# A PixArt block on one core: the MLP rows of batches 4 to 15 turned in 32x32 blocks by VectorE and regrouped through DRAM, a batch ahead, in place of TensorE transposes

## The chip, the core and the metric

The kernel runs on one core of a Trainium2 chip. The metric is the device time of one execution in microseconds (us). The kernel before takes 749.11 us (median of 3 runs, 748.86 to 749.24).

Engines are called as in the profile: PE is TensorE (matmuls; PEld its weight loads), DVE is VectorE, ACT is ScalarE, POOL is GpSimd, SP is SyncE, which here only issues DMAs.

## The reference

One transformer block on `x` of 16 batches x 256 tokens x 256 features: self-attention, cross-attention and an MLP, all in float32. The change lies in the MLP:

```
x_norm2 = modulate(_ln(x), shift_m, scale_m)      # t * (1 + scale) + shift, per batch and feature
h = jax.nn.gelu(x_norm2 @ W_mlp1 + b_mlp1)        # 256 -> 1024
h = h @ W_mlp2 + b_mlp2                           # 1024 -> 256
x = x + gate_m[:, None] * h
```

`_ln` takes mean and variance over the 256 features of a token.

## The kernel before

Every matmul operand is split into a high part in fp32r and a low part, the rest; a product is three matmuls (high x high, high x low, low x high). Attention takes the first 560 us or so. There the 32 units (16 self, 16 cross) run over a hand-written plan, and the result of each cross-attention goes to a DRAM tensor `x2d`. The rest is the MLP stage, the loop at the end of the function over `chunks`, 4 chunks `c` for each of 16 batches `b`. In the text, chunk number `i` is 4b + c, and a step is one pass of this loop.

What stands in a step, in order: `mlp_gelu` of chunk i+1 (ACT makes `hf` and `hh` from the PSUM tile `ph`, GELU in float32 and in fp32r; POOL makes `hl` = hf - hh); in steps 4b, for b from 2 to 14, `mlp_T(b+1)`; `mlp_first` of chunk i+2 (12 matmuls of 128x256 into `ph`, two PSUM buffers); `mlp_second` of chunk i-1 (12 matmuls into `s` or `st`: even batches use `s`, odd ones `st`). With the last chunk of a batch, `mlp_second` also has DVE multiply by the gate (`mt`), add the residual (`y`), and SP store `y` to `out`. So PE has 96 matmuls a batch, beside `mlp_T`.

`mlp_T(b)` of before: PE turns the normalised rows `xn_m` by 4 transposes (matmuls against the identity) into the PSUM tile `psT_m`; DVE scales and shifts them into `xTf_m` (2 instructions); ACT makes the high part `hi` from the same PSUM tile (2 instructions, into `wkch` or `wqch`, by turns); DVE subtracts to the low part `lo` (`wkcl` or `wqcl`). The first `mlp_first` that reads hi and lo of batch b+1 stands in step 4b+2.

The rows come there by `mlp_load` (SP reads x2d into `x`), `mlp_bias` (POOL adds `cb`), `mlp_stats` and `pow` (DVE statistics `st_m`, `mv_m`; POOL makes 1/sqrt, `rs_m`) and `mlp_apply` (DVE: (x - mean) * rs, 2 instructions, `xn_m`), spread over the steps of the batch two before. `mlp_residual` (DVE) makes `xmg`, `mlp_gates` (SP) loads the gate rows `gm`, the same 2 KB of DRAM to all 128 partitions.

What sets the order: PE, DVE, POOL and SP issue in the order of the code. ACT does so up to step 22 (`ACT.on = i < E_['AP']`, 23); behind that the scheduler places its instructions. Buffers of a tag are reused in turn: `x` has 5, `ph` 2, `hh` and `hl` 3.

Of the kernel before, what the change touches and what calls it, by code (L numbers as in the profile page):

```python
# [10 lines left out]
F32 = mybir.dt.float32  # L11
F32R = mybir.dt.float32r
AF = mybir.ActivationFunctionType
ALU = mybir.AluOpType
AX = mybir.AxisListType

P = 128
# [4 lines left out]
def pixart_block(  # L22
# [8 lines left out]
    B, N, H = x.shape  # L31
# [3 lines left out]
    NT = N // P  # L35
    KC = H // P
# [21 lines left out]
    ACT, DVE, POOL, SP = (InOrder(e, True) for e in (nc.scalar, nc.vector, nc.gpsimd, nc.sync))  # L58

    const = ctx.enter_context(tc.tile_pool(name="const", bufs=1))  # L60
    work = ctx.enter_context(tc.tile_pool(name="work", bufs=2))
    dram = ctx.enter_context(tc.tile_pool(name="dram", bufs=2, space=bass.MemoryType.DRAM))
    psum = ctx.enter_context(tc.tile_pool(name="psum", bufs=2, space=bass.MemoryType.PSUM))

    LONG, SHORT = "gen", "tr"
    ps_turn = [0]

    def ps_gen(name, tag=None):


        if tag is None and ps_turn[0] is not None:
            ps_turn[0] ^= 1
            tag = (SHORT, LONG)[ps_turn[0]]
        tag = tag or SHORT
        return psum.tile([P, 512], F32, tag=tag, name=name, bufs=2)
# [25 lines left out]
    def tok(ap, b):  # L101
        return ap[b].rearrange("(p t) h -> p t h", p=P)
# [24 lines left out]
    cpT = const.tile([P, 12, B], F32, name="cpT")  # L127
    bqkv = const.tile([P, 6, B], F32, name="bqkv")
    sc1 = const.tile([P, 2, 2, B], F32, name="sc1")
# [302 lines left out]
    def mm3_tok(dst, xT, t, W, kn=KC, start=True, stop=True):  # L432
        n = 0
        for k in range(kn):
            for a, b in ((xT[0], W[0]), (xT[0], W[1]), (xT[1], W[0])):
                PE.matmul(dst, a[:, k, t * P:(t + 1) * P], b[:, k],
                          start=(start and n == 0), stop=(stop and n == 3 * kn - 1))
                n += 1
# [134 lines left out]
    def bc_t(ap):  # L573
        return ap.unsqueeze(1).to_broadcast([P, NT, H])
# [113 lines left out]
    def side(home, r):  # L688
        return home[r] if isinstance(home, (list, tuple)) else home[:, r]
# [111 lines left out]
    M = {}  # L801

    def mlp_load(b):
        m = M[b] = M.get(b) or Box()
        if not hasattr(m, "h"):
            m.h, m.hT, m.kept = {}, {}, []
        m.xt = work.tile([P, NT, H], F32, tag="x" if b > 1 else "c", name=f"x2_{b}", bufs=5 if b > 1 else 2)
        SP.dma_start(m.xt, tok(X2d, b))
        m.ln = layernorm(lambda: m.xt, f"m{b}")

    def mlp_bias(b):
        POOL.tensor_tensor(M[b].xt, M[b].xt, bc_t(cb), ALU.add)

    def mlp_stats(b, power=False):
        M[b].ln.steps[0]()
        M[b].ln.steps[1](power)

    def mlp_apply(b):
        M[b].ln.steps[2]("dve")

    def mlp_gates(b):
        m = M[b]
        m.g = work.tile([P, 2, H], F32, tag="g", name=f"gm_{b}", bufs=3)
        SP.dma_start(m.g.rearrange("p a h -> p (a h)"),
                     gd[b, 2:4].rearrange("a h -> (a h)").partition_broadcast(P))

    def mlp_residual(b):
        m = M[b]
        m.xg = work.tile([P, NT, H], F32, tag="x1", name=f"xmg_{b}", bufs=7)
        DVE.tensor_tensor(m.xg, m.xt, bc_t(m.g[:, 1]), ALU.add)  # L830

    def mlp_T(b):

        m = M[b]
        pst = ps_gen(f"psT_m{b}", SHORT)
        for f in range(KC):
            for t in range(NT):
                PE.transpose(pst[:, f * N + t * P:f * N + (t + 1) * P],
                             m.ln.xn[:, t, f * P:(f + 1) * P], ident)
        y = work.tile([P, KC, N], F32, tag="y", name=f"xTf_m{b}", bufs=2)  # L840
        hi, lo = (Wkc, Wqc)[b % 2]
        for f in range(KC):
            DVE.tensor_scalar(y[:, f], pst[:, f * N:(f + 1) * N], sc1[:, 1, f, b:b + 1],
                              cpT[:, 6 + f, b:b + 1], ALU.mult, ALU.add)
        if b in E_['DV']:
            DVE.tensor_copy(hi, y)
        else:
            for f in range(KC):
                ACT.activation(hi[:, f], pst[:, f * N:(f + 1) * N], AF.Identity,
                               bias=cpT[:, 6 + f, b:b + 1], scale=sc1[:, 1, f, b:b + 1])  # L850
        DVE.tensor_tensor(lo, y, hi, ALU.subtract)
        m.xT = (hi, lo)
# [3 lines left out]
    def mlp_first(b, c):  # L856

        ph = ps_gen(f"ph_{b}_{c}", LONG).rearrange("p (j n) -> p j n", j=2)
        for j in range(2):
            mm3(ph[:, j], W1, 2 * c + j, M[b].xT)  # L860
        M[b].h[c] = ph
# [27 lines left out]
    def mlp_gelu(b, c):  # L889
        ph = M[b].h.pop(c)  # L890
        homes = (("pt", 5), ("qkh", 3), ("qkl", 3))
        if b == 0 and c:
            homes = (("x1", 7),) + (homes[1:] if c < 3 else (("xTh", 5), ("xTl", 5)))
        hf, hh, hl = [work.tile([P, 2, N], t, tag=tag, name=f"{n}_{b}_{c}", bufs=bufs)
                      for n, t, (tag, bufs) in zip(("hf", "hh", "hl"), (F32, F32R, F32R), homes)]
        for dst in (hf, hh):
            if c in M[b].kept:
                ACT.activation(dst, ph, AF.Gelu_apprx_tanh)
                continue
            for j in range(2):  # L900
                f = BM1 + 2 * c + j
                ACT.activation(dst[:, j], ph[:, j], AF.Gelu_apprx_tanh, bias=bT[:, f:f + 1])
        POOL.tensor_tensor(hl, hf, hh, ALU.subtract)
        M[b].hT[c] = (hh, hl)

    def mlp_second(b, c):
        m = M[b]
        hT = m.hT.pop(c)
        if c == 0:
            m.po = [side((sp, st)[b % 2], t)[:, :H] for t in range(NT)]  # L910
        for t in range(NT):
            mm3_tok(m.po[t], hT, t, [W2[0][:, 2 * c:2 * c + 2], W2[1][:, 2 * c:2 * c + 2]],
                    kn=2, start=(c == 0), stop=(c == NCH - 1))
        if c == NCH - 1:
            t1 = work.tile([P, NT, H], F32, tag="t1", name=f"mt_{b}")
            for t in range(NT):
                DVE.tensor_tensor(t1[:, t], m.po[t], m.g[:, 0], ALU.mult)
            y = work.tile([P, NT, H], F32, tag="x1", name=f"y_{b}", bufs=7)
            DVE.tensor_tensor(y, m.xg, t1, ALU.add)
            SP.dma_start(tok(out, b), y)  # L920


    W1 = [wself[:, 8 * i:8 * i + 8].rearrange("p (k c) h -> p k (c h)", k=KC) for i in range(2)]
# [98 lines left out]
    for p, f in zip(E_['M'], (mlp_load, mlp_bias, lambda b: mlp_stats(b, True), mlp_apply)):  # L1022
        end(p, f, 2)

    tail = []
    for i in range(3):
        b = i if i < 2 else 0
        u = ahead_of_mlp(nu + i, b)
        u.T, u.ln = [], []
        if i < 2:  # L1030
            u.ln = [layernorm(lambda b=b: M[b].xt, f"m{b}")]
            u.T = [transposed(lambda u=u: u.ln[0].xn, f"m{b}", [sc1[:, 1, f, b:b + 1] for f in range(KC)],
                              bias=[cpT[:, 6 + f, b:b + 1] for f in range(KC)])]
# [155 lines left out]
    last, o, q = units[-1], units[-1].post, units[-2].post  # L1189
    chunks = [(b, c) for b in range(B) for c in range(NCH)]  # L1190
    M[0].h[3] = tail[2].K.ps.rearrange("p (j n) -> p j n", j=2)
    for b in range(2):
        M[b].xT = M[b].src.xT
    mlp_gates(0)
    first_at = 7
    mlp_first(*chunks[first_at])
# [9 lines left out]
    o.turn(1)  # L1206
    o.norm(1)
    pst = {1: (lambda: mlp_T(2), o.aT.turn, o.aT.high, o.aT.low_dve), 4: (lambda: o.proj(0), lambda: o.proj(1), o.finish)}
    turns = {}
    turns.update((NCH * b, b + 1) for b in range(2, B - 1))  # L1210
    firsts = {5: 8}
    firsts.update((i, i + 2) for i in range(7, len(chunks) - 2))
    for i, (b, c) in enumerate(chunks):
        ACT.on = i < E_['AP']
        if 2 < i < len(chunks) - 1:
            mlp_gelu(*chunks[i + 1])
        if i in turns:
            mlp_T(turns[i])
        if i in firsts:
            mlp_first(*chunks[firsts[i]])  # L1220
        if i > 0:
            mlp_second(*chunks[i - 1])
        for f in pst.get(i, ()):
            f()
        ahead = b + 2 if 2 < b + 2 < B else None
        if c == 0 and ahead:
            mlp_bias(ahead)
        if c == 1:
            if b + 1 < B:
                mlp_gates(b + 1)  # L1230
            if ahead:
                mlp_stats(ahead)
            if b + 3 < B:
                mlp_load(b + 3)
        if c == 2 and ahead:
            M[ahead].ln.pow()
        if c == 3:
            if ahead:
                mlp_apply(ahead)
            mlp_residual(b)  # L1240
    mlp_second(*chunks[-1])


# [46 lines left out]
```

## Time and profile before

| | |
|---|---|
| median of 3 runs | 749.11 us (748.86 to 749.24) |
| the profiled execution | 746.75 us |
| its span, first to last instruction | 745.0 us |
| granted TensorE clock | 0.999 |
| PE busy | 734.8 us of the span |
| DVE, ACT, POOL busy | 578.8, 564.2, 490.1 us |
| DMA queue q1 (SP and ACT issue on it) | 78356 packets, 85.58 MB |

The profile is of one execution. In a row of a timeline the first two numbers are start and duration in us, then engine, line, operation and tiles, and in brackets how long the engine stood idle before and what it waited for. A row of a group has the count, then busy us, mean ns of one. All instructions show line 51, that of a helper, so tiles are what tells them apart. Matmuls overlap: a duration of 280 ns is a latency, and the step from start to start is what one costs.

### The profile page before, as it was taken

The numbers are of one execution on the slowest core, as the hardware profiler recorded it, in microseconds if no ns is written. First come the engines' busy times: TensorE is split into PE (matmuls) and PEld (weight loads), VectorE is DVE, ScalarE is ACT, GpSimd is POOL, SyncE is SP. The second block draws the span as 40 slices with busy tenths as digits, with TensorE's granted clock in tenths as the row PEclk, the third lists the DMA queues.
The fourth block names the chain that finished last, engine by engine and source line by source line (L and its number), as shares of the span: only waits on it lengthen the run. The fifth ranks groups of instructions, "written<-read, shape, count | busy, mean of one in ns | idle before, by whom it ended". The sixth has DMA issues, their size and how long they took to land.

```text
span 745.0 us, 25353 instructions
## 1 busy us (share of the span) xinstructions
PE 734.8 (99%) x10144; PEld 648.7 (87%) x10144; DVE 578.8 (78%) x1190; ACT 564.2 (76%) x978; POOL 490.1 (66%) x610
## 2 busy tenths in 40 slices
PE   9999999999999999999999999999999999999997
PEld 8778888888888888888888888878878999999997
DVE  4888898988888888888889888898726656666662
ACT  4278888888888888888888888888895666666663
POOL 6756676857667485765758678667566666666553
PEclk9999999999999999999999999999999999999999
DMA  6755445443644544454444545544213132221211
GB/s 207 200 147 153 133 126 143 123 130 100 171 120 128 146 117 145 109 165 128 136 142 123 158 129 160 153 115 126 70 59 100 49 80 70 61 85 43 85 45 43
DMA packets 78809, 87.98 MB, mean 118 GB/s; under 512 B 8610, under 2 KB 64196, under 8 KB 78692
## 3 DMA queue, kind: packets, MB, share of 16 engines
q1 hardware_dynamic: 78356, 85.58, 40.4%
q8 instruction: 80, 1.31, 0.8%
q0 software_dynamic: 192, 0.52, 0.3%
q10 hardware_dynamic: 144, 0.26, 0.2%
q14 instruction: 37, 0.30, 0.1%
HBM read 26.97 MB, written 8.46 MB: 48 GB/s over the span
## 4 chain that ended last, share of the span: by engine, by line
PE 95%; DVE 2%; issue 1%; POOL 1%; ACT 1%; POOLq 0%; DVEq 0%; ACTq 0%
PE s L51 18%; PE st L51 16%; PE o L51 16%; PE ph L51 11%; PE ps_qc L51 5%; PE ps_q L51 4%; PE ps_kc L51 3%; PE ps_P_s L51 3%; PE ps_v_s L51 3%; PE ps_v_c L51 3%; PE ps_k L51 3%; PE ps_P_c L51 2%; PE ps_h L51 1%; PE psT_q L51 1%; PE psA_c L51 1%; PE psT_m L51 1%
## 5 line engine op out<-in xcount | busy, mean ns | idle before, releaser
L51 DVE TENSOR_REDUCE mx<-s 128x2 f32<-128x512 f32 x504 | 324.8, 684 | 63.1 <-PE s L51 56.5
L51 ACT ACTIVATE pt<-st 128x1024 f32<-128x1024 f32 x252 | 258.8, 1027 | 17.7 <-PE st L51 11.7
L51 PE MATMUL s<-big 63*128 63x256 f32 (+1 forms) x1024 | 184.6, 298 | 0.5 <-DVE mx L51 0.4
L51 PEld LDWEIGHTS s<-big 63*128 63x128 f32 (+1 forms) x1024 | 133.8, 186 | 19.9 <-DVE l_kc L51 6.6
L51 PE MATMUL st<-big 64*128 64x256 f32 (+1 forms) x1024 | 134.3, 298 | 0.3 <-ACT pt L51 0.2
L51 POOL TENSOR_TENSOR hl<-hf,hh 128x512 fp32r<-128x512 f32 x64 | 84.0, 1315 | 66.2 <-ACT hh L51 66.2
L51 PE MATMUL o<-pt,v 128*32 128x256 f32 x2048 | 123.8, 382 | 0.0
L51 PEld LDWEIGHTS st<-big 64*128 64x128 f32 (+1 forms) x1024 | 96.1, 185 | 16.2 <-issue 12.9
L51 PEld LDWEIGHTS o<-pt,v 128*32 128x32 f32 x2048 | 60.0, 109 | 41.4
L51 ACT ACTIVATE hf<-ph,bT 128x256 f32<-128x256 f32 x114 | 47.8, 472 | 26.8 <-PE ph L51 26.8
L51 ACT ACTIVATE hh<-ph,bT 128x256 fp32r<-128x256 f32 x114 | 47.8, 471 | 24.2 <-PE st L51 12.8
L51 ACT COPY oT<-o 128x512 f32<-128x512 f32 x63 | 36.9, 585 | 32.8 <-PE o L51 32.8
L51 DVE TENSOR_SCALAR xn_m<-x,mv_m,rs_m 128x256 f32<-128x256 f32 x28 | 26.1, 973 | 38.0 <-POOL rs_m L51 38.0
L51 PE MATMUL s<-big,hh 128*128 128x256 f32 x256 | 46.8, 282 | 0.0
L51 PE MATMUL st<-big,hh 128*128 128x256 f32 x256 | 46.5, 281 | 0.0
L51 PE MATMUL ph<-wkch,wself 128*128 128x256 f32 x224 | 45.0, 284 | 0.0
L51 PE MATMUL ph<-wqch,wself 128*128 128x256 f32 x224 | 44.9, 284 | 0.0
L51 PE MATMUL ps_k<-xTh_s,wself 64*128 64x256 f32 (+1 forms) x232 | 43.8, 294 | 0.0
L51 PE MATMUL ps_q<-xTh_s,wself 64*128 64x256 f32 (+1 forms) x240 | 39.7, 283 | 0.4 <-DVE l_q L51 0.4
L51 PE MATMUL ps_v_s<-wself,xTh_s 64*128 64x256 f32 x224 | 39.2, 294 | 0.0
L51 PE MATMUL ps_P_s<-wself,xTh_as 64*128 64x256 f32 x256 | 39.0, 282 | 0.0
L51 PEld LDWEIGHTS st<-big,hh 128*128 128x128 f32 x256 | 39.0, 188 | 0.0
(245 smaller groups left out, 2469.2 us busy)
## 6 DMA issues: line engine op xcount, KB each, us to landing
big<-h_kc SPq DMA_DIRECT2D x64, 128.0 KB
big<-h_qc SPq DMA_DIRECT2D x64, 128.0 KB
big<-h_k SPq DMA_DIRECT2D x62, 128.0 KB
big<-h_q SPq DMA_DIRECT2D x62, 128.0 KB
big<-l_k SPq DMA_DIRECT2D x32, 128.0 KB
big<-l_q SPq DMA_DIRECT2D x32, 128.0 KB
g<-gd SPq DMA_DIRECT2D x16, 256.0 KB
c<-in_ctx_dram SPq DMA_DIRECT2D x16, 256.0 KB
```

What stands on the lines that cost most here:

```text
L51: i = f(*a, **k)
```

## The change

For batches 4 to 15 (`BY_DVE`) the transposes leave PE.

`mlp_apply(b)` writes `xn` with the features in four groups of 32 side by side, has DVE turn all of it in 32x32 blocks with one instruction (`STREAM_TRANSPOSE`, tile `blk_m`), and SP writes the blocks to a DRAM tensor `turned` by 4 DMAs; they go there in runs of 128 bytes (32 floats), 512 bytes from the start of one run to the next. `mlp_fetch(b)` reads them back by 4 DMAs of 32 rows of 2 KB into `raw_m`: features on partitions, tokens along the row. `mlp_T(b)` then has ACT scale and shift `raw_m` into `xTf_m`, and POOL make hi (a copy, CAST) and lo (subtract).

All of it stands about a batch sooner: apply of b+2 in step 4b and its fetch in step 4b+1, where apply stood in step 4b+3; bias of b+3 in step 4b+1, statistics and pow of b+3 in step 4b+2, the load of b+4 in step 4b+3 (batch 3 is loaded ahead of the loop).

In the last batch the residual is added and stored in two halves, the first by SP, the second by ACT.

```diff
+    BY_DVE = range(4, B)
+    turned = dram.tile([2, 32, 16, 4, 32], F32, name="turned", bufs=1)
     def mlp_apply(b):
-        M[b].ln.steps[2]("dve")
+        m = M[b]
+        if b not in BY_DVE:
+            m.ln.steps[2]("dve")
+            return
+        xn = work.tile([P, 4, KC, NT, 32], F32, tag="xn", name=f"xn_m{b}", bufs=3)
+        for t in range(NT):
+            DVE.tensor_scalar(xn[:, :, :, t], m.xt[:, t].rearrange("p (f g c) -> p g f c", f=KC, g=4),
+                              m.ln.mv[:, t, 0:1], m.ln.rs[:, t:t + 1], ALU.subtract, ALU.mult)
+        blocks = work.tile([P, 4, KC * NT, 32], F32, tag="A", name=f"blk_m{b}", bufs=1)
+        DVE.transpose(blocks.rearrange("p g x c -> p (g x c)"), xn.rearrange("p g f t c -> p (g f t c)"))
+        home = turned[b % 2]
+        for i in range(4):
+            SP.dma_start(home[:, :, i], blocks[32 * i:32 * i + 32].rearrange("p g x c -> p (g x) c"))
+    def mlp_fetch(b):
+        m, home = M[b], turned[b % 2]
+        m.raw = work.tile([P, KC, N], F32, tag="oT", name=f"raw_m{b}")
+        for g in range(4):
+            SP.dma_start(m.raw[32 * g:32 * g + 32].rearrange("p f n -> p (f n)"),
+                         home[:, 4 * g:4 * g + 4].rearrange("a x i c -> a (x i c)"))
...
+        if raw:
+            for f in range(KC):
+                ACT.activation(y[:, f], m.raw[:, f], AF.Identity,
+                               bias=cpT[:, 6 + f, b:b + 1], scale=sc1[:, 1, f, b:b + 1])
+            POOL.tensor_copy(hi, y)
+            POOL.tensor_tensor(lo, y, hi, ALU.subtract)
+            m.xT = (hi, lo)
+            return
...
+            for t, q in enumerate((SP, ACT)):
                 DVE.tensor_tensor(t1[:, t], m.po[t], m.g[:, 0], ALU.mult)
+                DVE.tensor_tensor(y[:, t], m.xg[:, t], t1[:, t], ALU.add)
+                q.dma_start(tok(out, b)[:, t], y[:, t])
...
+    mlp_load(3)
     mlp_gates(0)
...
+        if c == 0 and 2 < b + 2 < B and b + 2 in BY_DVE:
+            mlp_apply(b + 2)
...
+            if soon:
+                mlp_fetch(ahead)
+            if b + 3 in BY_DVE:
+                mlp_bias(b + 3)
...
+        if c == 2 and b + 3 in BY_DVE:
+            mlp_stats(b + 3)
+            M[b + 3].ln.pow()
...
+            if 4 <= b + 4 < B:
+                mlp_load(b + 4)
```

The first place is SP's queue in one batch late in the stage, before: the load of rows, the store of a result, the gate rows (numbers behind a name tell tiles apart).

```order
L51 DMA gm_14211<-gd 128x512
L51 DMA x_14_14220<-x2d 128x512
L51 DMA out_dram<-y_14342 128x512
L51 DMA gm_14379<-gd 128x512
L51 DMA x_15_14388<-x2d 128x512
```

And SP's queue at the same place of the changed kernel; `raw_m` is what `mlp_fetch` reads, `blk_m` the blocks that `mlp_apply` writes out.

```order
L51 DMA x_14_14189<-x2d 128x512
L51 DMA turned<-blk_m_14207 512x1x32 x4
L51 DMA out_dram<-y_14239 128x512
L51 DMA gm_14277<-gd 128x512
L51 DMA raw_m_14279<-turned 32x512 x4
L51 DMA x_15_14362<-x2d 128x512
```

The four writes stand ahead of the store of `y`, and the four reads behind the store and the gate rows: 11 DMAs a batch where there were 3.

The second place is ACT, where the scheduler placed `mlp_T` of one batch, before: the high part `wqch` from PSUM, behind both halves of chunk 1 (`hf_1`, `hh_1`).

```order
L51 ACTIVATE hf_0_14591<-ph_0_14564,bT 128x256 x2
L51 ACTIVATE hh_0_14592<-ph_0_14564,bT 128x256 x2
L51 ACTIVATE hf_1_14629<-ph_1_14599,bT 128x256 x2
L51 ACTIVATE hh_1_14630<-ph_1_14599,bT 128x256 x2
L51 ACTIVATE wqch<-psT_m_14637,cpT,sc_103 128x256 x2
```

And ACT in the changed kernel, `xTf_m` made from what the DMAs brought.

```order
L51 ACTIVATE hf_0_14327<-ph_0_14293,bT 128x256 x2
L51 ACTIVATE xTf_m_14372<-raw_m_14279,cpT,sc_103 128x256 x2
L51 ACTIVATE hh_0_14328<-ph_0_14293,bT 128x256 x2
L51 ACTIVATE hf_1_14364<-ph_1_14335,bT 128x256 x2
L51 ACTIVATE hh_1_14365<-ph_1_14335,bT 128x256 x2
```

The pair of `xTf_m` moved ahead of `hh_0` and of chunk 1. So it stands for batches 7, 9, 11, 13 and 15; for 8, 10, 12 and 14 one of the two stands ahead of `hh_0` and one behind it; for 4, 5 and 6 both stand behind `hh_1`.

The third place is POOL over one batch, before: four `hl`, the bias (`x<-x,cb`) and 1/sqrt (`rs_m`).

```order
L51 TENSOR_TENSOR hl_0_14259<-hf_0_14257,hh_0_14258 128x512
L51 TENSOR_TENSOR hl_1_14297<-hf_1_14295,hh_1_14296 128x512
L51 TENSOR_TENSOR x_14_14220<-x_14_14220,cb 128x512
L51 TENSOR_TENSOR hl_2_14348<-hf_2_14346,hh_2_14347 128x512
L51 TENSOR_TENSOR hl_3_14392<-hf_3_14390,hh_3_14391 128x512
L51 TENSOR_SCALAR rs_m_14387<-mv_m_14384 128x2
L51 TENSOR_TENSOR rs_m_14387<-rs_m_14387,mhalf 128x2
```

And POOL over one batch of the changed kernel.

```order
L51 TENSOR_TENSOR hl_0_14156<-hf_0_14154,hh_0_14155 128x512
L51 TENSOR_TENSOR hl_1_14193<-hf_1_14191,hh_1_14192 128x512
L51 CAST wkch<-xTf_m_14199 128x512
L51 TENSOR_TENSOR wkcl<-xTf_m_14199,wkch 128x512
L51 TENSOR_TENSOR hl_2_14246<-hf_2_14244,hh_2_14245 128x512
L51 TENSOR_TENSOR x_14_14189<-x_14_14189,cb 128x512
L51 TENSOR_TENSOR hl_3_14287<-hf_3_14285,hh_3_14286 128x512
L51 TENSOR_SCALAR rs_m_14324<-mv_m_14321 128x2
L51 TENSOR_TENSOR rs_m_14324<-rs_m_14324,mhalf 128x2
```

Two instructions, the CAST and the subtraction of the parts, came in between `hl_1` and `hl_2`, and the bias moved from ahead of `hl_2` to behind it.

More of the change, by code (lines that the diff above doesn't have):

```diff
@@ L834, in mlp_T @@
         m = M[b]
-        pst = ps_gen(f"psT_m{b}", SHORT)
-        for f in range(KC):
+        raw = b in BY_DVE
+        pst = m.raw.rearrange("p f n -> p (f n)") if raw else ps_gen(f"psT_m{b}", SHORT)
+        for f in range(0 if raw else KC):
             for t in range(NT):
@@ L915, in mlp_second @@
             t1 = work.tile([P, NT, H], F32, tag="t1", name=f"mt_{b}")
-            for t in range(NT):
+            y = work.tile([P, NT, H], F32, tag="x1", name=f"y_{b}", bufs=7)
+            if b < B - 1:
+                for t in range(NT):
+                    DVE.tensor_tensor(t1[:, t], m.po[t], m.g[:, 0], ALU.mult)
+                DVE.tensor_tensor(y, m.xg, t1, ALU.add)
+                SP.dma_start(tok(out, b), y)
+                return
+            for t, q in enumerate((SP, ACT)):
                 DVE.tensor_tensor(t1[:, t], m.po[t], m.g[:, 0], ALU.mult)
-            y = work.tile([P, NT, H], F32, tag="x1", name=f"y_{b}", bufs=7)
-            DVE.tensor_tensor(y, m.xg, t1, ALU.add)
-            SP.dma_start(tok(out, b), y)
+                DVE.tensor_tensor(y[:, t], m.xg[:, t], t1[:, t], ALU.add)
+                q.dma_start(tok(out, b)[:, t], y[:, t])
     W1 = [wself[:, 8 * i:8 * i + 8].rearrange("p (k c) h -> p k (c h)", k=KC) for i in range(2)]
@@ L1225, in pixart_block @@
         ahead = b + 2 if 2 < b + 2 < B else None
-        if c == 0 and ahead:
+        soon = ahead if ahead and ahead in BY_DVE else None
+        if c == 0 and ahead and ahead not in BY_DVE:
             mlp_bias(ahead)
@@ L1230, in pixart_block @@
                 mlp_gates(b + 1)
-            if ahead:
+            if soon:
+                mlp_fetch(ahead)
+            if b + 3 in BY_DVE:
+                mlp_bias(b + 3)
+            if ahead and not soon:
                 mlp_stats(ahead)
-            if b + 3 < B:
-                mlp_load(b + 3)
-        if c == 2 and ahead:
+        if c == 2 and ahead and not soon:
             M[ahead].ln.pow()
+        if c == 2 and b + 3 in BY_DVE:
+            mlp_stats(b + 3)
+            M[b + 3].ln.pow()
         if c == 3:
-            if ahead:
+            if ahead and not soon:
                 mlp_apply(ahead)
             mlp_residual(b)
+            if 4 <= b + 4 < B:
+                mlp_load(b + 4)
     mlp_second(*chunks[-1])
```

## The prediction

> **What bounds the kernel now.** I read the page, then busy times by window, the chain that ended last, PE's and SP's timelines in one batch, and the groups of the MLP stage.
>
> ```profile
> span 745.0 us, 25353 instructions
> ...
> PE 95%; DVE 2%; issue 1%; POOL 1%; ACT 1%; POOLq 0%; DVEq 0%; ACTq 0%
> ```
>
> PE carries 95% of the chain. Two batches of the MLP stage, cut from one store of `y` to the next (length, then busy us and counts of PE, PEld, DVE, ACT, POOL, the clock, DMA share, GB/s):
>
> ```profile
> 641.98:653.77 11.79, 11.79 (x102) 11.79 (x101) 7.66 (x14) 7.57 (x18) 7.34 (x7) 1.00 0.25 69
> 653.77:665.56 11.79, 11.79 (x102) 11.79 (x101) 7.66 (x14) 7.57 (x18) 7.35 (x7) 1.00 0.22 68
> ```
>
> A batch takes 11.79 us; PE never stands still; DVE, ACT and POOL have over 4 us free. The pace of matmuls alone is on the chain at the end, where no transposes are left:
>
> ```profile
> 727.39 1.42 PE ph L51 x12
> ...
> 733.06 1.42 PE ph L51 x12
> 734.48 5.68 PE st L51 x48
> ...
> 740.18 0.77 DVE mt L51 x2
> 740.95 0.02 issue
> 740.97 0.69 DVE y L51
> ```
>
> From 727.39 to 733.06 there are 48 matmuls in 5.67 us, 0.118 each; the 96 of a batch are 11.34.
>
> **What leaves PE.** The turn on PE's timeline:
>
> ```profile
> 647.44 0.28 PE L51 MATMUL st<-big,hl 128*128 128x256 f32 x1
> 647.56 0.60 PE L51 MATMUL psT_m<-ident,xn_m 128*128 128x128 f32 x4
> 647.91 0.36 PE L51 MATMUL ph<-wkch,wself 128*128 128x256 f32 x1
> 648.11 0.28 PE L51 MATMUL ph<-wkcl,wself 128*128 128x256 f32 x1
> ```
>
> From the start of the last `st` to the second `ph` it is 0.67 us, of which two matmuls are 0.24: four transposes cost 0.43. By the period it is 11.79 - 11.34 = 0.45. Twelve batches: 12 x 0.446 = **5.35 us** less. In the built program PE has 7433 rows for 7445, so the twelve groups do go. The question is what is late next.
>
> **DVE, POOL, ACT.** Groups of the stage (count, busy us, mean ns of one; the third and fourth are of the attention stage):
>
> ```profile
> L51 DVE TENSOR_SCALAR xn_m<-x,mv_m,rs_m 128x256 f32<-128x256 f32 x21 | 19.6, 973 | 25.8 <-POOL rs_m L51 25.8
> L51 DVE TENSOR_TENSOR wkcl<-xTf_m,wkch 128x512 fp32r<-128x512 f32 x5 | 6.9, 1377 | 5.7 <-ACT wkch L51 5.7
> L51 POOL TENSOR_TENSOR xTl_as<-y_as,xTh_as 128x512 fp32r<-128x512 f32 x16 | 20.7, 1292 | 1.4
> L51 POOL CAST xTh_as<-y_as 128x512 fp32r<-128x512 f32 x16 | 9.8, 612 | 25.7 <-ACT y_as L51 25.7
> L51 ACT ACTIVATE wqch<-psT_m,cpT,sc 128x256 fp32r<-128x256 f32 x12 | 6.1, 562 | 4.5 <-DVE xTf_m L51 4.5
> ```
>
> DVE loses two `xTf_m` and a `wkcl` or `wqcl` and gains the block transpose, which no row shows. I bound it by one pass over 512 elements, 0.69 us (the last `y`) to 1.38 (`wkcl`), and take the middle, 1.0; DVE's free time hides it. POOL gains 0.61 and 1.29: 7.35 + 1.90 = 9.25 of 11.34 us. Counting from the first `ph` of step 4b (time 0; 647.91 above): `hl_1` ends about 2.1, hi and lo by 4.1, and PE reads lo at 2 x 2.835 + 0.12 = 5.8. That hides them by 1.7 us; without the cover PE waits one for one. POOL then ends `hl_2` at 5.4, the bias at 6.7, `hl_3` at 8.0, pow at 9.0 to 10. ACT trades two instructions for two (0.56 each).
>
> **The way through DRAM.** SP in one batch, the DMA share (last but one column) behind it, and ACT:
>
> ```profile
> 653.77 0.34 SPq L51 DMA_DIRECT2D out_dram<-y  x1
> 654.16 0.43 SPq L51 DMA_DIRECT2D gm<-gd  x1
> 654.68 0.40 SPq L51 DMA_DIRECT2D x<-x2d  x1
> ```
>
> ```profile
> 653.77:654.60 0.83, 0.83 (x9) 0.83 (x8) 0.83 (x4) 0.78 (x2) 0.00 (x0) 1.00 0.00 0
> 657.50:658.50 1.00, 1.00 (x10) 1.00 (x10) 1.00 (x2) 0.37 (x2) 0.94 (x1) 1.00 0.37 137
> 658.50:659.50 1.00, 1.00 (x11) 1.00 (x10) 1.00 (x2) 0.48 (x3) 0.35 (x1) 1.00 0.00 0
> ```
>
> ```profile
> 655.29 0.84 ACT L51 ACTIVATE hf<-ph,bT 128x256 f32<-128x256 f32 x2 [0.64 <-PE ph L51]
> 656.65 0.84 ACT L51 ACTIVATE hh<-ph,bT 128x256 fp32r<-128x256 f32 x2 [0.52 <-PE s L51]
> ```
>
> Nothing moves in the first 0.83 us behind an issue, and the three DMAs are through by 658.5 at the latest, some 4.5 us behind the store's issue. The fetch stands in SP's queue where `x<-x2d` stood, behind the store and the gate rows, and brings the same 256 KB; so `raw_m` lands some 4.5 us behind the store's issue too. That store goes out at 5.86 now, because `y` waits for `wqcl`. With that gone, `mt` starts when PE is through, 2.84, and by the chain's rows `mt` and `y` take 1.48, at most 0.69 more beside POOL: issue at 4.3 to 5.0, `raw_m` there at 8.8 to 9.5, I take 9.1.
>
> When is it needed? `xTf_m` stands ahead of `hh_0`, ACT waits in order, and PE's `ph` at 11.34 needs the buffer that `hh_0` reads. So `xTf_m` must start by 11.34 - 0.84 - 1.05 = 9.45 in batches 7, 9, 11, 13, 15, and by 9.95 where one of the pair stands behind `hh_0`. **Slack 0.35 to 0.85 us**: covered, barely; each us beyond costs a us a batch, in the nine batches 7 to 15. Behind ACT, `hl_0` and PE's `mlp_second` wait too. I put 0.25 us in all for single misses.
>
> The four writes must have landed before the fetch goes, at 4.3 + 0.9 = 5.2 to 5.9; SP stands until they have, with the load of b+4 behind. DVE's apply starts at 9.0 to 10, takes twice 0.97, the transpose 1.0: writes issue at 0.6 to 1.6 of the next batch. No row shows 128-byte packets. Queue rows of the whole run and of the stage from 600 to 745 us (packets, MB, share of 16 engines):
>
> ```profile
> q1 hardware_dynamic: 78356, 85.58, 40.4%
> ```
>
> ```profile
> q1 hardware_dynamic: 4754, 8.65, 19.4%
> ```
>
> They give 0.404 x 16 x 745 / 78356 = 61.5 ns at 1092 bytes and 0.194 x 16 x 145 / 4754 = 94.7 ns at 1820. The line through both gives an estimate of 17.5 ns at 128 bytes; the upper bound is 61.5, and I take the line, since both rows move with size. 2048 packets are 128 an engine: 2.2 us, at most 7.9. With 0.83 at the start and 0.3 at the end the writes land at 3.9 to 4.9, ahead of the fetch.
>
> **Start and end.** Batch 3 still turns on PE, and PE waits for it:
>
> ```profile
> 569.28 1.74 POOL L51 TENSOR_TENSOR x<-x,cb 128x512 f32<-128x512 f32 x1
> 570.98 1.28 POOL L51 TENSOR_TENSOR hl<-hf,hh 128x512 fp32r<-128x512 f32 x1
> 572.75 1.30 POOL L51 TENSOR_TENSOR hl<-hf,hh 128x512 fp32r<-128x512 f32 x1 [0.49 <-ACT hh L51]
> 574.14 0.22 POOL L51 TENSOR_SCALAR rs_m<-mv_m 128x2 f32<-128x2 f32 x1
> ```
>
> ```profile
> 576.69 0.78 PE L51 MATMUL psT_m<-ident,xn_m 128*128 128x128 f32 x4 [0.63 <-DVE xn_m L51]
> ```
>
> The bias of batch 4, 1.3 us, now comes between the two `hl`; 0.49 of it fits the gap, so pow, apply and PE are 0.8 later: **+0.8 us** once (0 to 1.3). At the end four DVE instructions of about 0.4 replace 1.46 us, the last store goes out 0.1 later and is half as long (8 packets an engine, 0.3 us less): **-0.2** (-0.4 to +0.3).
>
> **Sum.** 745.0 - 5.35 + 0.8 - 0.2 + 0.25 = 740.5 us of span. The profiled execution took 746.75, 1.75 beyond its span, and the median of the runs, 749.11, lies 2.36 above that. I carry the difference of -4.5 over: **744.6 us**.
>
> **Rivals.** *The writes are slow, and the kernel is slower.* For it: 128-byte runs have no row. At 61.5 ns they land at 9.6 to 10.6, the four reads add 3.5 (four issues, 0.83, the data): 13.6, some 3.9 behind the 9.7 of the average batch. The chain begins a batch earlier, so a wait there moves the deadline as well, and half falls to each of 11 batches: +21 us, 766. It decides from 0.8 us late (half of it, 11 times, is 4.5), that is 38 ns a packet: no change, 749. The Trainium skill, "DMA: Bandwidth & Descriptors", Specifications, says that transfers below 512 bytes make the DMA engine read, modify and write; taken as twice the line's cost that is 35 ns, an estimate, 0.5 us late and 747.3, and no run here shows it yet. Against: the trace's packets cost by their size. Chance 0.15.
>
> *The reads are late behind the gate rows.* Four DMAs of 32 rows may land 1 to 1.5 us later than one of 128: 0.4 to 0.9 beyond the deadline, nine times: 748.2 to 752.7. For: slack is 0.35. Chance 0.11.
>
> *POOL becomes the bound.* If DVE stretches all six long instructions of a batch by 0.45 (1.74 above for 1.29), POOL needs 11.95 of 11.34, 0.6 x 12: 751.8. Most rows stand at 1.29. Chance 0.04.
>
> **Numbers.** Forecast 0.70. Of the first rival 0.10 is slower and 0.05 no change; of the second 0.05 faster, 0.03 none, 0.03 slower; of the third 0.01, 0.01, 0.02. Under 0.2%, 1.5 us, a measurement here hardly tells from no change. Faster 0.76, same 0.09, slower 0.15. The range goes from no loss at the start and the best end (749.11 - 5.75, and 0.45 for the spread of runs) to the no-change cases: 742.9 to 749.1.
>
> **What would show it.** Right: windows of 11.3 to 11.4 us a batch with PE full, ACT's `xTf_m` with no long wait, lo ready 1 us ahead of `ph`, the last `psT_m` wait near 1.4. Wrong: ACT waiting at `xTf_m` for a DMA and PE idle at `ph` for ACT (writes late if SP waits at the fetch, reads late if not), or PE waiting for `wkcl`. Twelve times 0.45 missing with PE full would say that the transposes were hidden.

## The result and the profile after

The changed kernel takes 753.07 us (median of 8 runs, 750.94 to 754.51), the kernel before beside it 748.40 us (8 runs, 747.33 to 750.43). The ratio is 1.0058, 95% interval 1.0041 to 1.0075: slower by 0.6%, and above the predicted range. The profiled execution took 750.94 us, the quickest of the eight, with a span of 749.2 for the 745.0 of before. Its chain of waits:

```profile
span 749.2 us, 25393 instructions
...
PE 88%; DMA 3%; DVE 3%; ACT 2%; issue 2%; SPq 1%; POOL 1%; ACTq 0%; POOLq 0%; DVEq 0%
```

PE carried 95% of the chain of before; now `raw_m` by DMA, SP's queue and ACT hold parts of it. What PE waited for in the MLP stage (us in total, times, longest):

```profile
PE ph L51 <- ACT hh L51: 8.0, 8, 2.4
PE psA_c L51 <- DVE oT L51: 1.1, 1, 1.1
PE psT_m L51 <- DVE xn_m L51: 0.4, 1, 0.4
```

PE waits eight times at `ph` for `hh`. One batch of the changed kernel, on SP, ACT and PE:

```profile
665.55 0.36 SPq L51 DMA_DIRECT2D out_dram<-y  x1
665.96 0.43 SPq L51 DMA_DIRECT2D gm<-gd  x1
666.62 1.71 SPq L51 DMA_DIRECT2D raw_m<-turned  x4
668.37 0.42 SPq L51 DMA_DIRECT2D x<-x2d  x1
```

```profile
668.55 0.84 ACT L51 ACTIVATE hf<-ph,bT 128x256 f32<-128x256 f32 x2 [0.64 <-PE ph L51]
671.81 1.09 ACT L51 ACTIVATE xTf_m<-raw_m,cpT,sc 128x256 f32<-128x256 f32 x2 [2.42 <-DMA raw_m<-turned]
672.81 0.82 ACT L51 ACTIVATE hh<-ph,bT 128x256 fp32r<-128x256 f32 x2
```

```profile
672.48 0.28 PE L51 MATMUL st<-big,hl 128*128 128x256 f32 x1
673.68 0.39 PE L51 MATMUL ph<-wkch,wself 128*128 128x256 f32 x1 [0.92 <-ACT hh L51]
```

The store goes out at 665.55 and ACT can start on `raw_m` at 671.81, 6.26 us later (one of the later batches of the table below). Until then ACT stands at `xTf_m` (2.42 us); `hh`, whose input has long been there, stands behind it, and PE waits 0.92 for the buffer that `hh` reads. SP issued these reads without a wait and went on; in the whole stage it stood for the writes once, 0.3 us. That is the sign that the prediction named for "the reads are late", not "the writes are late".

A wait costs more than its length. Three groups of 12 matmuls on the chain, the first two behind a wait, the third undisturbed:

```profile
648.97 1.68 PE ph L51 x12
...
661.15 1.69 PE ph L51 x12
...
664.26 1.42 PE ph L51 x12
```

Each of the eight groups behind a wait takes 0.27 us more. By PE's rows 0.16 of it is a matter of counting: a wait is counted from the end of the last matmul, 0.28 us behind its start, where the next one would have started 0.12 behind it. The other 0.11 is the second matmul, which starts 0.23 us behind the first for 0.12 (648.97 and 649.20 in the first of these groups). Eight waits are 8.0 + 8 x 0.27 = 10.2 us. From the last turn on PE, `psT_m` (576.69 before, 575.83 now), to the end of its matmuls (740.16 and 744.20) the kernel takes 4.90 us more: -5.35 for the transposes and +10.2 is +4.8. So the transposes did go, and what came instead is these waits.

### The profile page after: what moved, and what is told of

It reads as the page before. It is cut to its first block, busy times and chain, and to the rows that moved or that the text cites. A ratio compares the mean times of both kernels' runs of the same rounds, so it can differ in the third digit from the quotient of the medians.

```text
span 749.2 us, 25393 instructions
## 1 busy us (share of the span) xinstructions
PE 731.0 (98%) x10096; PEld 643.1 (86%) x10096; DVE 554.0 (74%) x1167; ACT 563.2 (75%) x978; POOL 519.4 (69%) x634
## 4 chain that ended last, share of the span: by engine, by line
PE 88%; DMA 3%; DVE 3%; ACT 2%; issue 2%; SPq 1%; POOL 1%; ACTq 0%; POOLq 0%; DVEq 0%
PE s L51 17%; PE o L51 15%; PE st L51 14%; PE ph L51 9%; PE ps_q L51 5%; PE ps_qc L51 4%; PE ps_kc L51 3%; PE ps_v_c L51 3%; PE ps_P_s L51 3%; PE ps_k L51 3%; PE ps_v_s L51 2%; PE ps_P_c L51 2%; DMA raw_m<-turned 2%; SPq L51 1%; PE ps_h L51 1%
## 5 line engine op out<-in xcount | busy, mean ns | idle before, releaser
L51 POOL TENSOR_TENSOR hl<-hf,hh 128x512 fp32r<-128x512 f32 x64 | 87.1, 1364 | 40.4 <-ACT hh L51 40.1
L51 PEld LDWEIGHTS ph<-wkch,wself 128*128 128x128 f32 x224 | 36.3, 189 | 6.2 <-ACT hh L51 6.1
L51 POOL CAST xTh_c<-y_c 128x512 fp32r<-128x512 f32 x16 | 9.8, 612 | 43.0 <-ACT y_c L51 43.0
L51 PEld LDWEIGHTS ph<-wqch,wself 128*128 128x128 f32 x224 | 36.3, 189 | 3.5 <-ACT hh L51 3.5
```

The costliest lines, as they stand in the source:

```text
L51: i = f(*a, **k)
```

## The experiments

Theory A: `raw_m` is late because of what stands ahead of it in the queue, and the price comes through ACT's order. Its rivals: the four reads are slow by themselves (B), parts that come late cost PE directly (C), the writes are late.

**1. The reads ahead of the gate rows.**

```diff
+            if soon:
+                mlp_fetch(ahead)
             if b + 1 < B:
                 mlp_gates(b + 1)
-            if soon:
-                mlp_fetch(ahead)
```

> The one edit: SP issues the four reads of raw_m right behind the store, ahead of the gate rows. Theory A (the reads stand in the queue behind 128 reads of one gate row, and share it with the load of x behind them): raw_m, which now lands 5.3 to 6.2 us behind the store's issue, lands 3.7 to 4.5 behind it, the waits of PE at ph for hh (8.0 us in 8 places, and 0.27 us of restart at each) go, and the span falls from 749.2 to 739.3 to 741, the time to 741 to 743. Theory B (the four reads are slow by themselves: four issues and rows 8 KB apart): only the issue of the gate rows, 0.5 to 0.8 us, is saved, about half of the stall stays, the time is 745 to 748.

Measured: 744.19 us, 0.9961 of the kernel before (0.9948 to 0.9974), span 743.6: between the ranges of A and B. PE's waits in the stage:

```profile
PE ph L51 <- ACT hh L51: 2.3, 3, 1.1
```

Most of the stall is gone, but not all. The edit also moved ACT's instructions: the scheduler put both `xTf_m` ahead of `hh_0` in all of batches 7 to 15, where four were split, so `raw_m` is asked for sooner in those four and the gain doesn't come from ACT's order. Two batches of this kernel tell why, the store on SP and `xTf_m` on ACT:

```profile
663.04 0.34 SPq L51 DMA_DIRECT2D out_dram<-y  x1
...
675.49 0.34 SPq L51 DMA_DIRECT2D out_dram<-y  x1
```

```profile
668.34 1.09 ACT L51 ACTIVATE xTf_m<-raw_m,cpT,sc 128x256 f32<-128x256 f32 x2 [2.21 <-DMA raw_m<-turned]
679.46 1.10 ACT L51 ACTIVATE xTf_m<-raw_m,cpT,sc 128x256 f32<-128x256 f32 x2 [1.03 <-DMA raw_m<-turned]
```

5.30 us behind the store in one, 3.97 in the other. The DMA queues in the window 663.04 to 668.3 (packets, MB, share of 16 engines):

```profile
q1 hardware_dynamic: 477, 0.79, 52.0%
q8 instruction: 1, 0.02, 1.0%
```

A load of instructions, one packet of 16 KB, took one of the 16 DMA engines for 0.8 to 0.9 us (0.010 x 16 x 5.26); the window of the other batch has no row for q8. These loads come every 13 to 18 us in the stage. The table below takes batches with one apart. The three waits of PE that are left are in the three batches with a load between 1 and 5 us behind the store.

**2. The reads ahead of the store: not what was made.** The fetch was put ahead of `mlp_second` in step 4b+1; the store stands in step 4b, so SP's order came out as in the first experiment.

> The one edit: SP issues the four reads of raw_m ahead of the store as well, as soon as the four writes have landed (some 3.7 us behind their first issue, by 11 ns a packet). Theory A: raw_m lands 1 us or more ahead of the deadline in every batch, no wait of ACT at xTf_m, the time 741 to 743, as for the first edit or 0.5 better. Theory B: also no stall left, 741 to 743, since the start is over 2 us earlier; so this run and the first one differ under B and not under A. If the store is held up by it, the last wait of DVE or SP shows it, and the time doesn't move, for no one on the path waits for a store.

Measured: 745.06 us, 0.9966 (0.9954 to 0.9979): a repeat of the first, which it confirms, and no test of B. The eighth does what was meant.

**3. ACT in the order of the code.**

```diff
-'AP': 23
+'AP': 64
```

> The one edit: ScalarE's program order is kept in the whole MLP stage, so xTf_m stands behind hh_1 in batches 7 to 15 as it does in 4 to 6; the reads are as late as before. Theory A and B (the price comes only through ACT, which stands in order at xTf_m with hh_0 behind it): PE has no wait, the span is 739 to 741, the time 741 to 743, with raw_m still 5.3 to 6.2 us behind the store. Rival C (the late rows cost PE by the parts as well, wkcl late for ph): the wait moves to PE ph for wkcl or wqcl and the time stays above 746.

Measured: 742.10 us, 0.9932 (0.9919 to 0.9944), span 739.7. Two batches (columns as in the prediction) and, of one of them, SP and ACT:

```profile
627.54:638.88 11.34, 11.34 (x99) 11.34 (x98) 6.39 (x11) 7.58 (x20) 9.90 (x10) 1.00 0.43 118
638.88:650.21 11.33, 11.33 (x99) 11.33 (x98) 5.95 (x11) 7.57 (x20) 9.88 (x10) 1.00 0.47 116
```

```profile
627.54 0.36 SPq L51 DMA_DIRECT2D out_dram<-y  x1
627.95 0.43 SPq L51 DMA_DIRECT2D gm<-gd  x1
628.61 1.72 SPq L51 DMA_DIRECT2D raw_m<-turned  x4
```

```profile
634.15 0.84 ACT L51 ACTIVATE hh<-ph,bT 128x256 fp32r<-128x256 f32 x2 [0.52 <-PE s L51]
634.88 1.09 ACT L51 ACTIVATE xTf_m<-raw_m,cpT,sc 128x256 f32<-128x256 f32 x2
```

A batch takes 11.34 us with PE full: the forecast, reached. The reads stand where they stood; `xTf_m` now starts 7.3 us behind the store and, from batch 5 on, waits for nothing. Of ACT's instructions in the stage only the `xTf_m` changed places. So the whole price came through two ACT instructions a batch (one of them in the split batches) that the scheduler had put ahead of `hh_0`. C falls: `xTf_m`, and the parts behind it, are later here than in the changed kernel, and PE waits at no `ph`.

**4. Gate rows from 128 different rows.**

```diff
-                     gd[b, 2:4].rearrange("a h -> (a h)").partition_broadcast(P))
+                     X2d[b].rearrange("(p t) h -> p (t h)", p=P))
```

> The one edit: gm is filled by a load of 128 different rows of 2 KB of x2d in place of 128 reads of one row (the gates are left out, so the output isn't the reference's); same size, same place in the queue. Theory A1 (the reads of one row slow the queue): the packets of gm take some 84 ns instead of up to 640, raw_m lands about 1 us sooner, half to all of the stall goes: 742 to 746. Theory A2 (only the bytes ahead and beside count): no change, 750 to 754.

Measured: 746.87 us, 0.9993 (0.9980 to 1.0006), 3.6 us of span less than the changed kernel. ACT can start on `raw_m` 0.5 to 0.9 us sooner in the mean (table), with ACT's order as in the changed kernel, and PE's waits are 3.8 us in 6 places. So A1 holds in part: 128 reads of one row hold the queue up longer than 128 rows do. The place behind the 256 KB costs about as much: from here to the first experiment it is another 0.5 to 1.0 us.

**5. ACT in order, and batch 3 by VectorE too** (`BY_DVE = range(3, B)`).

> The order of ScalarE kept in the whole MLP stage, as in the third experiment (0.9932 of the kernel before), and batch 3 turned by VectorE too. Theory A: PE sheds 0.43 us of transposes and the 0.4 us that it waits at psT_m for xn_m of batch 3: 0.8 us better than the third experiment, 0.992 of the kernel before. Rival: batch 3 is made while the last attention work still holds DVE and POOL; raw_m comes too late for PE's first ph of batch 3, and the time is the third experiment's or up to 3 us above it (0.993 to 0.997).

Measured: 744.35 us, 0.9961 (0.9946 to 0.9975), the rival. Batch 3's first `ph` in this kernel:

```profile
585.79 0.35 PE L51 MATMUL ph<-wqch,wself 128*128 128x256 f32 x1 [3.20 <-ACT hh L51]
```

**6. The load of x ahead of the writes.** `mlp_load(b + 4)` moves from step 4b+3 to step 4b, ahead of `mlp_apply`.

> The changed kernel with one edit: the load of x for batch b+4 goes out ahead of the four writes, not right behind the four reads. If an engine takes its packets in the order of issue, what stands behind the reads doesn't slow them: raw_m is ready 5.3 to 5.9 us behind the store's issue as before (6.3 to 7.2 where a 16 KB instruction load falls into the window), and the time stays at 1.004 to 1.008 of the kernel before. If the load behind shares the engines with the reads, 4.5 to 5.0 us, and the time falls to 0.996 to 1.000.

Measured: 754.52 us, 1.0096 (1.0061 to 1.0130). The clock was 0.990 to 0.997 in its four runs, and in the profiled one the part before the MLP, which the edit doesn't touch, was 5.6 us longer, so the time says little. The table says more: ACT starts 5.53 us behind the store without an instruction load, 5.58 in the changed kernel, with the same order on ACT. What stands behind the reads didn't slow them.

**7. The rest of the change alone** (`BY_DVE` empty: PE turns every batch; the earlier load of x and the halves at the end stay).

> The rest of the change alone: PE turns all batches as before, no block transpose, no writes and reads; x is loaded for b+4 in step 4b+3 and the last batch goes out in halves. My sum for the end is -0.2 us (-0.4 to +0.3), the start costs nothing without the earlier bias: 0.999 to 1.0005 of the kernel before. If the moved load of x costs something by itself (statistics waiting for it), it is slower by up to 3 us, with DVE st_m waiting for a DMA.

Measured: 747.68 us, 1.0002 (0.9990 to 1.0013): nothing to be seen, as expected.

**8. The reads right behind the writes** (`mlp_fetch(b + 2)` behind `mlp_apply(b + 2)` in step 4b).

> The changed kernel with one edit: the four reads stand right behind the four writes in SP's queue, ahead of the store, the gate rows and the load (in the second experiment they stood behind the store all the same, so it was the first one again). The writes land 2.15 us behind each issue, so the reads go out 0.5 to 1.5 us before the store did, with nothing else in the queue. Theory A: raw_m is ready 1 us or more ahead of the deadline, an instruction load of 0.9 to 1.3 us beside it is covered too, PE has no wait at ph: 739.5 to 741 us of span, 0.992 to 0.994 of the kernel before, 2 us better than the first experiment. If SP standing at the reads delays the store and the loads to where someone waits for them (x late for the bias, POOL or DVE waiting for a DMA), 0.995 to 1.00.

Measured: 747.14 us, 0.9987 (0.9970 to 1.0005), span 743.9. The expectation failed; SP in one batch:

```profile
613.03 2.58 SPq L51 DMA_DIRECT2D turned<-blk_m  x4
617.26 1.72 SPq L51 DMA_DIRECT2D raw_m<-turned  x4
```

The reads wait for the writes and go out 4.23 us behind the first of them; the first experiment's trace has the reads of the same batch at 617.37. With the store out of the way the writes hold the reads, and they go out no sooner. The time is worse than the first experiment's by 0.26%, and this run doesn't show why: the scheduler put both `xTf_m` ahead of `hf_0` as well in batches 7 to 15, so ACT asks for `raw_m` sooner, and the place in SP's queue is not the only thing that changed. Only where the order on SP is changed does this matter: in the changed kernel SP waited for the writes once, 0.3 us.

**9. One read, behind the gate rows.** The DRAM copy is laid out so that one read of 128 rows of 2 KB does, and the writes are runs of 512 bytes.

```diff
-    turned = dram.tile([2, 32, 16, 4, 32], ...)
+    turned = dram.tile([2, 4, 32, 4, 4, 32], ...)
-            SP.dma_start(home[:, :, i], blocks[...].rearrange("p g x c -> p (g x) c"))
+            SP.dma_start(home[:, :, i].rearrange("g a x c -> a g (x c)"), blocks[...].rearrange("p g x c -> p g (x c)"))
-        for g in range(4):
-            SP.dma_start(m.raw[32 * g:32 * g + 32]..., home[:, 4 * g:4 * g + 4]...)
+        SP.dma_start(m.raw.rearrange("p i f t c -> p (i f t c)"), home.rearrange("g a i x c -> (g a) (i x c)"))
```

> The changed kernel with another layout of the DRAM copy: the writes are 512-byte runs in place of 128, and raw_m comes with one read of 128 rows in place of four of 32; its place in SP's queue, behind the gate rows, is kept, and ACT reads raw_m through a view of 32-element runs. If the four issues (1.71 us, one takes 0.42) are what makes raw_m late, it is ready 1.3 us sooner, 4.0 to 4.6 us behind the store, and only batches with an instruction load of 16 KB in the window stall: 0.995 to 0.998 of the kernel before. If the 128 reads of one gate row ahead set it (they land 4.0 us behind their own issue), raw_m gains 0.5 us at most: 1.000 to 1.003.

Measured: 755.00 us, 1.0097 (1.0077 to 1.0117), above both forecasts. Three issues fewer bring 0.2 us: behind the gate rows the number of reads hardly matters. It isn't a clean test of the number alone: the runs of the writes changed too, and the scheduler now put both `xTf_m` ahead of `hh_0` in all of batches 7 to 15, where four were split, which asks for `raw_m` 0.5 us sooner in those four, and PE waits 9.9 us in 9 places for 8.0 in 8. The part before the MLP took 2.6 us more in its profiled execution as well (first store of the stage at 571.87 for 569.25).

**10. One read, ahead of the gate rows** (9 and 1 together).

> Both: one read, and it goes out right behind the store, ahead of the gate rows; ScalarE's order is left as in the changed kernel. By the first experiment's 3.9 us behind the store (no instruction load beside it) less 1.3 for three issues, raw_m is ready 2.6 to 3 us behind the store, 4 us with an instruction load: within the 5 us that there are in every batch. No wait of PE at ph, 739.5 to 740.5 us of span, 0.992 to 0.994 of the kernel before, as with ScalarE's order kept. If not, the writes bind it (SP waiting for them), 0.996 to 0.999 as in the eighth.

Measured: 741.17 us, 0.9913 (0.9895 to 0.9932), span 739.1. The scheduler orders ACT here, but not as in the changed kernel, which the expectation took for granted: both `xTf_m` stand ahead of `hf_0` in batches 7, 9, 11, 13 and 15 and ahead of `hh_0` in the four others, all at least as early as there. SP and ACT in one batch:

```profile
661.51 0.36 SPq L51 DMA_DIRECT2D out_dram<-y  x1
662.09 0.34 SPq L51 DMA_DIRECT2D raw_m<-turned  x1
```

```profile
664.89 1.10 ACT L51 ACTIVATE xTf_m<-raw_m,cpT,sc 128x256 f32<-128x256 f32 x2 [1.60 <-DMA raw_m<-turned]
```

3.38 us behind the store; ACT waits 8.9 us in the stage, and PE at `ph` not once. Against the first experiment that is 0.8 us sooner without an instruction load, so B holds in part: ahead of the gate rows four reads do cost more than one. This is the fastest version, not to be told from the third by these intervals.

**11. One read ahead, ACT in order, batch 3 by VectorE.**

> One read ahead of the gate rows, ScalarE's order kept, and batch 3 turned by VectorE too. In the fifth experiment raw_m of batch 3 came 3.2 us too late; 1.3 us fewer for the issues and 1.0 to 1.6 for the gate rows leave 0.3 to 0.9 us of it, against 0.8 us that PE saves there: 0.991 to 0.9935 of the kernel before. If batch 3 is bound by its writes and not by the reads, PE still waits 2 to 3 us at that ph and it is 0.995 to 0.997.

Measured: 741.23 us, 0.9916 (0.9896 to 0.9936). PE waits 1.3 us at batch 3's `ph` (0.86 for `hh`, 0.46 for `wqcl`), which takes back what its turn saves.

The table: time from the store's issue to the start of `xTf_m`, over the batches from 7 on in which ACT waited there; "load" is an instruction load that begins 1 to 5 us behind the store and ahead of that start. The last column is PE at `ph` for `hh`.

| kernel | mean without load (batches) | mean with load (batches) | PE: us, times |
|---|---|---|---|
| changed | 5.58 (6) | 6.76 (3) | 8.0, 8 |
| 6, load of x moved | 5.53 (6) | 6.66 (3) | 7.2, 9 |
| 9, one read behind gates | 5.37 (7) | 6.34 (2) | 9.9, 9 |
| 4, gates from own rows | 5.11 (6) | 5.91 (3) | 3.8, 6 |
| 1, reads ahead of gates | 4.15 (6) | 5.37 (3) | 2.3, 3 |
| 10, one read ahead | 3.35 (5), 4.18 with one at 0.2 us | 3.36 (1) | 0 |

## Why the prediction was wrong

**The failed step** is the landing of `raw_m`: "so `raw_m` lands some 4.5 us behind the store's issue too", and with it "slack 0.35 to 0.85 us: covered, barely". ACT could start on it 5.58 us behind the store in the mean, 6.76 with an instruction load beside it. The mechanism of the loss was on the list, as the second rival ("the reads are late behind the gate rows", 748.2 to 752.7), with a chance of 0.11; its size was nearly right (0.4 to 0.9 us in nine batches; measured 8.0 us in eight) and lacked the 0.27 of each restart. Where the missing 1.1 to 2.3 us come from:

- 4.5 was read from one batch, the one at 653.77, and the trace of before had others. Two rows of SP and one window, of before:

```profile
618.41 0.34 SPq L51 DMA_DIRECT2D out_dram<-y  x1
618.79 2.04 SPq L51 DMA_DIRECT2D gm<-gd  x1
```

```profile
623.00:624.00 1.00, 1.00 (x11) 1.00 (x10) 1.00 (x2) 0.60 (x2) 0.49 (x1) 1.00 0.73 260
```

At 4.6 to 5.6 us behind that store the engines still moved 260 GB/s; an instruction load began 0.5 us behind it, and SP's issue of the gate rows took 2.04 us for 0.43. By the last packets, the three DMAs of a batch were through at 4.6 to 5.8 us in eleven batches of before, 4.9 in the mean; where the slack is 0.35 to 0.85, the spread decides, and one batch, one of the quickest, doesn't show it.
- "Through" is not yet usable, a step that the prediction put at nothing. In the next to last fetch of the changed kernel (store at 702.51) nothing stands behind the reads; its last packet ends 5.07 us behind the store, and ACT starts on `raw_m` 0.60 us after that, at 708.18:

```profile
706.51:707.58 1.07, 1.07 (x11) 1.07 (x10) 0.19 (x1) 0.00 (x0) 0.98 (x2) 1.00 0.36 126
707.58:708.18 0.60, 0.60 (x7) 0.60 (x6) 0.57 (x2) 0.00 (x0) 0.00 (x0) 1.00 0.00 0
```

The same fetch of the ninth experiment, one read, has 0.36 us from its last packet to ACT:

```profile
711.44:711.80 0.36, 0.36 (x5) 0.36 (x5) 0.07 (x1) 0.00 (x0) 0.25 (x1) 1.00 0.00 0
```

With 4.9 for the packets that gives 5.3 us, near the 5.37 of that kernel; it is an estimate for the other batches, in which other packets follow at once.
- Four reads in place of one cost 0.2 us behind the gate rows (9) and 0.8 ahead of them (1 and 10). The 0.35 between the batch that was read and the mean, the 0.36 from last packet to use and these 0.2 are 0.9 of the 1.1 us without a load; the last 0.2 stays open.
- In three of nine batches an instruction load goes with 1.2 us more. The Trainium skill, "DMA: Bandwidth & Descriptors", Queues, rings and completion order, says that an engine takes its queues in turn by whole packets; the trace fits that, since one packet of 16 KB takes one of the 16 engines for 0.9 to 1.2 us in these batches. That `raw_m` waits for that very engine is inferred; no run shows it.
- The store was inside its range of 4.3 to 5.0 us in one parity (665.55, 4.40 behind the first `ph` at 661.15) and above it in the other (654.25, 5.28 behind 648.97), where `y` ran beside POOL; 0.27 of both is the restart of PE:

```profile
652.90 1.33 DVE L51 TENSOR_TENSOR y<-xmg,mt 128x512 f32<-128x512 f32 x1
...
664.75 0.77 DVE L51 TENSOR_TENSOR y<-xmg,mt 128x512 f32<-128x512 f32 x1
```

**The steps that held.** The transposes are worth what was said: 11.34 us a batch in the third and tenth experiments, 5.0 and 6.2 us under the kernel before. The writes were in time, the first rival's case did not come: SP's issues and the DMA window 660.9 to 665.2 of the changed kernel,

```profile
660.87 2.57 SPq L51 DMA_DIRECT2D turned<-blk_m  x4
```

```profile
q1 hardware_dynamic: 2112, 0.26, 35.3%
```

give 0.353 x 16 x 4.3 / 2112 = 11.5 ns a packet (64 of them are semaphores), under the estimate of 17.5. SP takes 0.65 us to issue each of the four, so their issue is longer than their packets (128 a DMA engine, 1.5 us in all). The Trainium skill ("DMA: Bandwidth & Descriptors", Specifications) says that below 512 bytes a DMA engine reads, modifies and writes. The 35 ns that the prediction estimated from that sentence did not come; whether the engine reads and modifies, no run shows. The block transpose takes 0.71 us for the 1.0 assumed, and POOL is no bound:

```profile
L51 DVE STREAM_TRANSPOSE blk_m<-xn_m 128x512 f32<-128x512 f32 x10 | 7.1, 712 | 0.3
```

**Two small terms had the wrong sign.** The start was to cost 0.8 us. POOL's pow did come 0.7 later against the work ahead of it, but DVE's apply of batch 3, beside POOL's short pow in place of an `hl`, took 0.74 us for 1.68; of both kernels, before first:

```profile
575.18 1.68 DVE L51 TENSOR_SCALAR xn_m<-x,mv_m,rs_m 128x256 f32<-128x256 f32 x2 [3.16 <-POOL rs_m L51]
```

```profile
575.27 0.74 DVE L51 TENSOR_SCALAR xn_m<-x,mv_m,rs_m 128x256 f32<-128x256 f32 x2 [1.38 <-POOL rs_m L51]
```

The wait at `psT_m` is 0.40 for 0.63; that the apply is quicker because of POOL is read from this one pair of rows. The halves at the end cost 0.2 instead of bringing it: on the chain they take 1.71 us, 744.20 to 745.91, for 1.48.

```profile
744.22 0.44 DVE mt L51
...
745.48 0.43 DVE y L51
```

## What to carry to other kernels

A wait put ahead of other work on an engine that issues in order is paid by what stands behind it: here two ACT instructions a batch cost PE 10 us over the stage, and one number that keeps the order of the code turned a loss of 0.6% into a gain of 0.7%. Where the slack of a DMA is under a microsecond, take its landing from all batches of the trace, not from one, take it where the reader starts and not where the packets end, and count every DMA ahead of it in the queue. An edit to one queue can move the instructions that the scheduler places on another engine; read their order again in every run. The reader's data goes to the front of the queue, in one DMA; gate rows that no one needs for a while go behind it.

## What the runs showed of the hardware

- A load of instructions (one packet of 16 KB, every 13 to 18 us in this stage) took one DMA engine for 0.9 to 1.2 us in the late batches of the changed kernel. Where one began 1 to 5 us behind the store, `raw_m` was usable 0.8 to 1.2 us later in five kernels; in the tenth experiment, where one began 2.89 us behind it, `raw_m` was not late (3.36). No run took these loads away; it rests on the batches with and without one.
- From the last packet of a read to the start of the ACT instruction that waits for it: 0.5 to 0.9 us with four reads (the changed kernel and the sixth experiment), 0.36 and 0.45 with one (the ninth), in batches with nothing behind the reads.
- Packets of 128 bytes took 11.5 ns each, and each of the four writes took SP 0.65 us to issue where a read of 32 rows took 0.42.
- 128 reads of one row are slower than of 128 rows: 0.5 to 0.9 us for what stands behind them.
- What stands behind a DMA in the same queue didn't slow it (5.53 and 5.58 us, the sixth experiment).
- After each of the eight waits, 0.4 to 2.4 us, the second matmul started 0.11 us later than usual, at an undiminished clock (1.00).
